# A decoder layer on one core: even key and value projections, self values by token tiles, output parts fetched three ahead

## The chip, the core and the metric

The kernel runs on one core of a Trainium2 chip. The metric is device time in microseconds from the start to the end of one execution; the median of several executions is compared. A core has five engines with a queue of instructions each, worked off in order: TensorE (PE in the profile; its weight loads are the row PEld), VectorE (DVE), ScalarE (ACT), GpSimd (POOL) and SyncE (SP). SP computes nothing here: it issues nearly all DMAs, and a DMA that has to wait for a buffer holds up all DMAs behind it on that queue.

## The reference, cut to what matters

One layer: self attention, cross attention, a mixture of experts, each added to its input and normalised. 16 sequences of 100 tokens, width 512, all in float32.

```python
x = layernorm(x + self_attention(x))             # 16 heads of 32, causal, softmax
x = layernorm(x + cross_attention(x, context))   # 16 query heads of 128, 4 key/value heads,
                                                 # context 16 x 361 x 512, q and k rms-normalised
x = layernorm(x + moe(x))                        # router picks 2 of 8 experts (512 x 512, silu), projection, rms norm
```

## The kernel before, in words

**Products.** Large float32 matrices are held as a pair, a rounded high part and the rest. `mm3` (lines 145 to 147) computes one product as three: high x high, low x high, high x low. `mmk` runs it over the four 128-row pieces of a 512-wide contraction, so that one 128 x 512 result costs 12 matmuls. `split` (lines 132 to 141) makes a pair: ACT (or DVE) casts the high part, DVE or POOL subtracts to get the low part.

**Order.** The program is written in one order, but a scheduler places each engine's instructions by its own estimate of times; it can move work of a later stage forward as soon as the memory of its tiles is free. Tiles come from pools that are opened and closed; a pool opened after others have been closed reuses their memory, and an instruction that writes into it waits until the last reader of what lay there before is done. `in_turn` and `keep_in_program_order` pin some instructions.

**Self attention** (0 to about 207 us): four groups of 4 sequences (400 tokens), 4 units of 4 heads in each group, 16 units in all. `self_v` computes values with one `mmk` for each sequence (100 tokens as weights, 512 columns), copies them by ACT from the accumulator to `V[g, r]`, and `self_attend` uses those as weights. The dictionary `extra`, filled by `at(unit, step, ...)`, puts other work between the steps of a unit: projections of the next units, values of the next group (units 2 and 3 of a group), splits of weight rows, and at the end the first output projections (`b_fetch`, `b_split`, `b_out`, `b_xT`; five tiles before the stage closes).

**Query stage** (about 207 to 440 us): output projection of self attention, layernorm, queries for cross attention, stored to DRAM (`qd`).

**Cross attention** (about 440 to 1087 us): 16 sequences x 4 key/value heads g, 64 units. A unit computes scores of the next unit (`x_scores`: three products of 362 columns for each of 4 heads, softmax over DVE, ACT, DVE, POOL), transposes its own probabilities in three chunks (`x_turn`) and multiplies them with the values (`x_attend`). Beside it `kv_project(b + 1, g)` projects keys and values of the next sequence, one chunk of 128 context rows in each of units g = 0, 1, 2; unit 3 has none. Keys are rms-normalised and transposed (`kv_turn`), values split into a spare weight slot. In every third unit a row of the output weights is fetched (`f_wo`) and split at once (`load_row`). The result goes to DRAM as `od`.

**Output projection of cross attention** (`acc`): 52 parts (13 tiles of 128 tokens x 4 heads g); `d_part` multiplies the four query heads of a part with 512 rows of output weights, 12 matmuls. `d_load(i + 1)` fetches the next part's `of` from `od` into pool `d_in` (two buffers) and splits it right away, one part ahead of its use. The last three tiles are done head by head. Between the parts lie `d_norm` (add, layernorm, store), `d_turn` (transposes for the router), `d_logits`, the routing (`choose`, `settle`, `slots`, on DVE and with small products), and `load_expert`, which fetches and splits the four rows of an expert's weights in one go, at parts 8, 16, 24 and 32 and for the other experts when a slot of output weights comes free.

**Experts and end**: `e_gather` collects tokens by an indirect DMA on POOL into the four `xs` buffers of pool `k_x` (`xsp`), which is opened after the attention's pools have been closed; then expert products, the final projection and norms.

Of the kernel before, what the change touches and what calls it, by code (L numbers as in the profile page):

```python
# [9 lines left out]
FP = mybir.dt.float32  # L10
# [7 lines left out]
B, S, D = 16, 100, 512  # L18
# [10 lines left out]
GB = 4  # L29
NG = B // GB  # L30
GT = GB * S
TT = [(t, min(128, T - t)) for t in range(0, T, 128)]
EPS_LN = 1e-5
EPS_RMS = 1e-6
# [28 lines left out]
def tile_decoder_layer(  # L63
    ctx: ExitStack,
    tc: tile.TileContext,
    x: bass.AP,
    xT: bass.AP,
    ctxT: bass.AP,
    mask: bass.AP,
    wqT: bass.AP,  # L70
# [25 lines left out]
    def pool(stack, name, bufs=1, **k):  # L96
        return stack.enter_context(
            tc.tile_pool(name=name, bufs=bufs, reuse_waits="tile", **k)
        )
# [124 lines left out]
    w1 = pool(a_l, "a_1", 1)  # L224
    w2 = pool(a_l, "a_2", 2)
    w3 = pool(a_l, "a_3", 8)
    ps.append(pool(a_l, "ps_a", 2, space=PSUM))
    ps_s = pool(a_l, "ps_s", 1, space=PSUM)

# [68 lines left out]
        split(*chunk("q", c), nc.scalar, nc.gpsimd)  # L298
        split(*chunk("k", c), nc.scalar, nc.gpsimd)

    def self_v(g, r):
        pv = bank("mm" if g else "t", [S, D], f"pv_{g}_{r}")
        mmk(
            pv,
            lambda k: xg[g][:, k, r * S : (r + 1) * S],
            lambda k: units["wv_s"][:, k, :],
        )
        V[g, r] = w1.tile([S, D], FP, name=f"v_{g}_{r}", tag="v", bufs=8)
        nc.scalar.copy(V[g, r], pv)

    def self_q(g, c):
        cc = slice(c * 128, (c + 1) * 128)
# [84 lines left out]
    def self_attend(g, c):  # L397

        av = bank("t", [128, GB, S], f"av_{g}_{c}")
        prev = None  # L400

        for r in range(GB):
            for j in (3, 0, 1, 2):
                h = c * 128 + 32 * j
                ins = nc.tensor.matmul(
                    av[32 * j : 32 * j + 32, r, :],
                    V[g, r][:, h : h + 32],
                    PT[g, c, j][:, r, :],
                    start=True,
                    stop=True,  # L410
                    tile_position=(0, 32 * j),
                )
                prev = in_turn(ins, prev)
        o = w2.tile([128, GT], FP, name=f"o_{g}_{c}", tag="o")
        nc.scalar.copy(o, av.rearrange("p r s -> p (r s)"))
        nc.sync.dma_start(o1d[g][:, c], o)
# [57 lines left out]

    ROW = {}

    def fetch_row(name, s, src, k):
        units[name] = slot_of(s)
        f = stage.tile([128, D], FP, name=f"f_{name}_{k}", tag="f")
        tc.keep_in_program_order(nc.sync.dma_start(f, src[:, k]))  # L480
        ROW[name, k] = f

# [11 lines left out]
    for u, (g, c) in enumerate(heads4):  # L494
        if u + 2 < NU:
            if u < 2:
                at(u, 0, split_chunk, u + 2)
            at(u, 0, self_k, *heads4[u + 2])
            at(u, 2, self_q, *heads4[u + 2])
        if g + 1 < NG:  # L500
            if c == 0:
                at(u, 1, fetch_x, g + 1)
                for k in range(2):
                    at(u, 3, split_x, g + 1, k)
            if c == 1:
                for k in range(2):
                    at(u, 1, split_x, g + 1, 2 + k)
            if c > 1:
                for r in range(2):
                    at(u, 1 + 2 * r, self_v, g + 1, 2 * (c - 2) + r)  # L510

    rows = [("wo_s", 3, kp(woT), k) for k in range(KC)]
    rows += [("wq_0", 4, Wqg[0], k) for k in range(KC)]
# [12 lines left out]
        at(i // 4, i % 4, behind, split_row, "wq_3", k)  # L526

    AHEAD = 5
    at(10, 0, b_open)
    for t, i in enumerate((44, 48, 52, 54, 58)):  # L530
        at(i // 4, i % 4, b_fetch, t)
        i += 2 if t == AHEAD - 1 else 4
        at(i // 4, i % 4, behind, b_split, t)
    for t, i in enumerate((51, 55, 59, 61, 62)):
        at(i // 4, i % 4, b_out, t)
    for t, i in enumerate((57, 60, 63)):
        at(i // 4, i % 4, b_xT, t)
# [1 line left out]
    self_q(0, 0)  # L539
    self_k(0, 0)  # L540
    self_scores(*heads4[0])
    self_v(0, 0)
    split_chunk(1)
    for r in range(1, GB):
        self_v(0, r)
    self_q(0, 1)
    self_k(0, 1)
    for u, unit in enumerate(heads4):
# [134 lines left out]

    spare = [slot_of(s)[:, k] for s in (4, 5) for k in range(KC)]

    def kv_project(b, i):
        c0, n = CH[i]
        if i == 0:
            K[b] = pair(w2, [128, NKV, SP], f"kT_{b}", tag="kT")
            nc.gpsimd.memset(K[b].h[:, :, SE:].bitcast(FP), 0.0)  # L690
            nc.gpsimd.memset(K[b].l[:, :, SE:].bitcast(FP), 0.0)
        ct = CT.pop((b, i))
        m = b * len(CH) + i
        pk = bank("mm", [128, D], f"pk2_{b}_{i}")
        mmk(pk[:n], lambda k: ct[:, k, :n], lambda k: wk[:, k, :])
        ks = w0.tile([128, D], FP, name=f"ks_{b}_{i}", tag="ks")
        nc.vector.tensor_tensor(ks[:n], pk[:n], bk_bc[:n], ALU.add)
        pv = bank("mm", [128, D], f"pv2_{b}_{i}")
        mmk(pv[:n], lambda k: ct[:, k, :n], lambda k: wv[:, k, :])
        VS[b, i] = spare[m % 6]  # L700
        split(VS[b, i][:n], pv[:n])
        kr = ks[:n].rearrange("p (h d) -> p h d", d=HD2)
        ss = small.tile([128, NKV], FP, name=f"kss_{b}_{i}", tag="kss")
        sq = w0.tile([128, HD2], FP, name=f"ksq_{b}_{i}", tag="sq", bufs=1)
        for h in range(NKV):
            nc.vector.tensor_tensor_reduce(
                out=sq[:n],
                in0=kr[:, h, :],
                in1=kr[:, h, :],
                scale=1.0,  # L710
                scalar=0.0,
                op0=ALU.mult,
                op1=ALU.add,
                accum_out=ss[:n, h : h + 1],
            )
        rs = rms_scale(ss[:n], n, NKV, f"k_{b}_{i}")
        nc.gpsimd.tensor_tensor(
            kr, kr, rs[:n].unsqueeze(2).to_broadcast([n, NKV, HD2]), ALU.mult
        )
        KS[b, i] = kr  # L720

    def kv_turn(b, i):
        c0, n = CH[i]
# [74 lines left out]
    for i in range(len(CH)):  # L798
        if i == 2:
            split_ctx(0, 2)  # L800
        kv_project(0, i)
        kv_turn(0, i)
    x_load(0, 1)
    for h in range(GR):
        x_scores(0, 0, h)
    order = [(b, g) for b in range(B) for g in range(NKV)]
    OT, X1 = {}, {}

    def d_open():
        kv_l.close()  # L810
        inp["d"] = pool(d_i, "d_in", 2)

    TAIL = 3
    parts = [(t, g) for t in range(NT - TAIL) for g in range(NKV)]
    parts += [(t, g) for g in range(NKV) for t in range(NT - TAIL, NT)]

    def d_load(i):
        t, g = parts[i]
        n = TT[t][1]
        p = inp["d"]  # L820
        of = p.tile([128, GR, 128], FP, name=f"of_{t}_{g}", tag="of")
        nc.sync.dma_start(of[:, :, :n], od[t][:, g * GR : (g + 1) * GR, :n])
        OT[t, g] = pair(p, [128, GR, 128], f"ot_{t}_{g}", tag="ot")
        split(OT[t, g][:, :, :n], of[:, :, :n], low=nc.vector if i % 2 else nc.gpsimd)

    def d_part(i, among={}):

# [34 lines left out]
    for i, (b, g) in enumerate(order):  # L862
        if b == B - 1:
            if g == 0:
                d_open()
                d_load(0)
            for j in range(HEAD * g, HEAD * (g + 1)):
                d_load(j + 1)
                d_part(j)
                if parts[j][1] == NKV - 1:  # L870
                    d_norm(parts[j][0])
        if b + 1 < B:
            if g == 0:
                fetch_ctx(b + 1)
                split_ctx(b + 1, 0)
            if g < len(CH):
                kv_project(b + 1, g)
            if g + 1 < len(CH):
                split_ctx(b + 1, g + 1)
        if i + 2 < len(order):  # L880
# [24 lines left out]
    ctx.enter_context(fin)  # L905
    k1 = pool(fin, "k_1", 1, side="right")
    xsp = pool(fin, "k_x", 4, side="right")
    gs = ExitStack()
    gw = pool(gs, "gate", side="right")
    d_l = ExitStack()  # L910
# [423 lines left out]

    raw = w1.tile([128, 2, D], FP, name="raw")

    def load_expert(e, last=False):
        for k in range(KC):
            if last and k > 1:
                f = raw[:, k - 2]  # L1340
            else:
                f = stage.tile([128, D], FP, name=f"f_e_{e}_{k}", tag="f")
                tc.keep_in_program_order(nc.sync.dma_start(f, kp(expert_w[e])[:, k]))
            split(
                slot_of(e)[:, k],
                f,
                nc.vector if last and k == 1 else nc.scalar,
                nc.vector if last and k else nc.gpsimd,
            )

    for i in range(HEAD * NKV, len(parts)):
        t, g = parts[i]
        if i + 1 < len(parts):
            d_load(i + 1)
        among = {}
        if t < NT - TAIL:
            if g == 1:
                d_turn(t - 1)
            if g == 3:
                among = d_logits(t - 1)  # L1360
            if g == 0 and t in (2, 4, 6, 8):
                load_expert(early[t // 2 - 1])
        elif t > NT - TAIL and g == 0:
            if t < NT - 1:
                d_turn(NT - TAIL - 1)
# [5 lines left out]
        if g == NKV - 1:  # L1371
            with tc.high_priority(offset=URGENT if t >= NT - TAIL else 0):
                d_norm(t)
        if t == NT - 1 and g < NKV - 1:
            load_expert(wo_slot[g])
        if (t, g) == (CUT, 0):
            nc.sync.dma_start(raw, kp(expert_w[wo_slot[3]])[:, 2:])
        if t % 3 == 0 and t <= CUT and g == 3:
# [3 lines left out]
        if (t, g) == (CUT, 3):  # L1382
            settle(0, CUT)
            slots(0, EARLY, CUT)
        if (t, g) == (NT - 1, 1):
            for k in range(4):
                e_gather(k)
    d_i.close()
    ck_l.close()
    load_expert(wo_slot[3], True)  # L1390
    e_turn(0)
    e_turn(1)
    e_product(0, d_logits(NT - TAIL))
# [436 lines left out]
```

## Time and profile before

| | us |
|---|---|
| median of 6 runs | 1415.05 (1411.93 to 1422.0) |
| profiled execution, its time | 1421.13 |
| its span, first to last instruction | 1419.3 |
| PE busy in the span | 1340.7 (94%) |
| DVE, ACT, POOL busy | 938.9, 757.5, 713.3 |
| mean granted clock of PE | 0.972 |

How to read it: times are those of one execution. A matmul is pipelined: its record is longer than the distance to the next one's start, so that a sum of records is more than the time they take. In a row of a timeline the bracket at the end says how long the engine sat idle before the instruction, and what ended that wait. In a row of waits stand the waiting engine and line, what it waited for, then the sum in us, how often, and the longest. In a table of stretches each engine has its busy time and, in brackets, its number of instructions; PEclk is the mean granted clock in that stretch.

### The profile page before, as it was taken

The page shows a single profiled execution, that of the slowest core. Times are in us where ns is not written, and L with a number is a line of the kernel's source. Part 1 is how long each engine was busy: PE and PEld are TensorE (multiplying, and loading weights), DVE is VectorE, ACT ScalarE, POOL GpSimd, SP SyncE. Part 2 cuts the span into 40 slices and gives each one's busy share as a digit, 9 for nine tenths or more (in the row PEclk, how much of TensorE's full clock was granted, in tenths as well). Part 3 has the DMA queues.
Part 4 walks back from the last instruction along what each step waited for, and adds up shares of the span by engine and source line. Part 5 has one row for each costly group of instructions (what it writes and reads, how often), then busy time and mean ns, then how long its engine had stood idle before and what let it go on. Part 6 is the DMA issues. An engine that isn't in the chain of part 4 may idle for free.

```text
span 1419.3 us, 25131 instructions
## 1 busy us (share of the span) xinstructions
PE 1340.7 (94%) x7952; PEld 1111.7 (78%) x7952; DVE 938.9 (66%) x2932; ACT 757.5 (53%) x1899; POOL 713.3 (50%) x839
## 2 busy tenths in 40 slices
PE   8999989999999999999999999999999898998895
PEld 7888868887778888888888778888888675686783
DVE  5776577766456777777677676776754557764587
ACT  4666653444445666666566556666654233333356
POOL 6877663344245555555455455554554445532630
PEclk9999989999999999999999999999999999899997
DMA  5231254555552223333333123322445554678874
GB/s 158 72 93 52 72 155 120 120 96 110 97 102 66 47 66 74 70 78 69 76 69 76 43 64 77 76 64 55 105 106 159 189 163 149 194 230 242 261 243 144
DMA packets 197872, 159.79 MB, mean 113 GB/s; under 512 B 133322, under 2 KB 152878, under 8 KB 197742
## 3 DMA queue, kind: packets, MB, share of 16 engines
q1 hardware_dynamic: 187904, 137.83, 37.1%
q0 software_dynamic: 4576, 14.95, 3.6%
q10 hardware_dynamic: 5262, 5.41, 1.3%
q8 instruction: 65, 1.06, 0.3%
q14 instruction: 65, 0.53, 0.1%
HBM read 107.16 MB, written 50.99 MB: 111 GB/s over the span
## 4 chain that ended last, share of the span: by engine, by line
PE 63%; DVE 13%; DMA 13%; ACT 5%; issue 3%; POOL 2%; SPq 1%; ACTq 0%; DVEq 0%; POOLq 0%
PE pv L145 4%; PE pv L146 4%; PE pv L147 3%; PE ptp L767 3%; PE pk L145 3%; PE pk L147 3%; PE pk L146 3%; DMA qd<-qTb 3%; PE s L145 3%; PE pq L145 3%; PE pq L147 3%; PE pq L146 3%; DMA f_wo<-in_Wo 3%; PE s L147 3%; PE s L146 2%
## 5 line engine op out<-in xcount | busy, mean ns | idle before, releaser
L759 POOL TENSOR_SCALAR p<-p,sums 100x361 f32<-100x361 f32 x256 | 146.5, 576 | 103.4 <-DVE sums L758 92.3
L746 DVE CUSTOM_DVE_ANT_0 p<-s,nmask 100x361 f32<-100x361 f32 x256 | 133.1, 527 | 67.4 <-PE s L147 59.1
L757 ACT ACTIVATE p<-p,nm 100x361 f32<-100x361 f32 x256 | 153.1, 601 | 40.1 <-DVE nm L746 36.8
L140 DVE TENSOR_TENSOR pT_l<-ptp,pT_h 128x400 fp32r<-128x400 f32 (+1 forms) x192 | 107.5, 568 | 56.4 <-ACT pT_h L137 55.8
L145 PE MATMUL pq<-WH 128*128 128x512 f32 (+2 forms) x272 | 107.1, 394 | 5.5 <-DVE WH L139 5.5
L767 PE MATMUL ptp<-ident,p 100*128 100x100 f32 (+1 forms) x768 | 107.2, 251 | 0.0
L137 ACT CAST pT_h<-ptp 128x400 fp32r<-128x400 f32 (+1 forms) x192 | 91.2, 486 | 29.7 <-PE ptp L767 29.1
L767 PEld LDWEIGHTS ptp<-ident,p 100*128 100x128 f32 (+1 forms) x768 | 95.3, 151 | 13.2 <-POOL p L759 2.3
L140 POOL TENSOR_TENSOR cT_l<-cf,cT_h 128x512 fp32r<-128x512 f32 (+1 forms) x48 | 54.3, 1132 | 100.2 <-ACT cT_h L137 98.2
L146 PE MATMUL pq<-WL,WH 128*128 128x512 f32 (+2 forms) x272 | 104.5, 384 | 0.0
L147 PE MATMUL pq<-WH,WL 128*128 128x512 f32 (+2 forms) x272 | 104.2, 383 | 0.0
L147 PE MATMUL acc<-WH,ot_l 128*128 128x512 f32 (+1 forms) x208 | 86.3, 416 | 7.8 <-DVE ot_l L140 6.2
L145 PE MATMUL acc<-WH,ot_h 128*128 128x512 f32 (+1 forms) x208 | 85.8, 413 | 6.7 <-ACT ot_h L137 6.7
L145 PE MATMUL s<-kT_h,WH 128*100 128x362 f32 x256 | 88.3, 355 | 2.1 <-ACT kT_h L137 2.1
L145 PE MATMUL av<-pT_h,WH 128*128 128x400 f32 (+1 forms) x192 | 77.2, 402 | 12.2 <-ACT pT_h L137 11.7
L147 PE MATMUL s<-kT_h,WL 128*100 128x362 f32 x256 | 84.8, 331 | 0.0
L146 PE MATMUL acc<-WL,ot_h 128*128 128x512 f32 (+1 forms) x208 | 84.5, 406 | 0.0
L146 PE MATMUL s<-kT_l,WH 128*100 128x362 f32 x256 | 84.2, 329 | 0.0
L614 POOL TENSOR_TENSOR qs<-qs,r_q 128x512 f32<-128x512 f32 (+1 forms) x52 | 54.0, 1068 | 58.9 <-DVE r_q L169 47.7
L140 POOL TENSOR_TENSOR WL<-qf,WH 128x400 fp32r<-128x400 f32 x64 | 67.3, 1051 | 31.2 <-ACT WH L137 27.7
L145 PE MATMUL pv<-WH,cT_h 128*128 128x512 f32 (+1 forms) x192 | 79.7, 415 | 1.3 <-DVE WL L140 1.3
L145 PE MATMUL pk<-WH,cT_h 128*128 128x512 f32 (+1 forms) x192 | 78.3, 408 | 0.3
(337 smaller groups left out, 4012.6 us busy)
## 6 DMA issues: line engine op xcount, KB each, us to landing
qf<-qd SPq DMA_DIRECT2D x64, 200.0 KB, 3.1
of<-od SPq DMA_DIRECT2D x48, 256.0 KB, 3.8
cf<-in_ctxT SPq DMA_DIRECT2D x16, 722.0 KB, 4.3
eb<-in_expert_b SPq DMA_DIRECT2D x32, 256.0 KB, 4.4
ysd<-h SPq DMA_DIRECT2D x32, 256.0 KB, 4.5
f_e<-in_expert_w SPq DMA_DIRECT2D x30, 256.0 KB, 4.6
f_wq<-in_Wq SPq DMA_DIRECT2D x16, 256.0 KB, 3.4
f_wo<-in_Wo SPq DMA_DIRECT2D x16, 256.0 KB, 4.8
```

The source lines that it names most:

```text
L137: ins = nc.scalar.copy(dst.h, src)
L140: low.tensor_tensor(dst.l, src, dst.h.bitcast(FP), ALU.subtract)
L145: nc.tensor.matmul(out, a.h, b.h, start=start, stop=False)
L146: nc.tensor.matmul(out, a.h, b.l, start=False, stop=False)
L147: nc.tensor.matmul(out, a.l, b.h, start=False, stop=stop)
L614: nc.gpsimd.tensor_tensor(qr[:, hs, :], qr[:, hs, :], rs[:n, hs].unsqueeze(2).to_broadcast([n, GR, HD2]), ALU.mult,)
L746: nc.vector.tensor_tensor_reduce(out=p, in0=sc[:, :SE], in1=nmask, scale=1.0, scalar=BIG, op0=ALU.add, op1=ALU.min, accum_out=nm,)
L757: nc.scalar.activation(p, p, AF.Exp, bias=nm, scale=-1.0, accum_out=sh)
L759: nc.gpsimd.tensor_scalar(p, p, sh, 1.0, ALU.mult, ALU.mult)
L767: nc.tensor.transpose(pt[:n, h, :], probs[h][:, c0 : c0 + n], ident[:S, :S])
```

## The change

Three parts.

1. *Self values by token tiles.* For groups 1 to 3 a group's 400 tokens are taken as three tiles of 128; the remaining 16 tokens of the three groups (48 in all, a new input `xlT`) are projected in one go. As sequences begin at multiples of 100, rows of a tile are then moved by DMA into the `V[g, r]` that they belong to. Group 0 stays as it was. To keep the pool `a_x` open, `b_open` and the first output fetches move from unit 10 and 11 to unit 12.
2. *Even projections.* `kv_project` is cut into `k_project` and `v_project`. Keys of the next sequence stay at g = 0, 1, 2; values go to g = 0, 2, 3.
3. *Output parts and expert rows.* `d_load` is cut into `d_fetch` (the DMA) and `d_load` (the split). After attention the fetches run three parts ahead, in the `xs` buffers of `xsp`. Expert rows are fetched up to four ahead (in `stage` and in the buffers of `d_in` that the parts no longer use) and split one by one, every second part. The first gathers are issued from part 48 instead of 45.

```diff
-    def self_v(g, r):
-        pv = bank("mm" if g else "t", [S, D], f"pv_{g}_{r}")
-        mmk(pv, lambda k: xg[g][:, k, r * S : (r + 1) * S], lambda k: units["wv_s"][:, k, :])
-        V[g, r] = w1.tile([S, D], FP, name=f"v_{g}_{r}", tag="v", bufs=8)
-        nc.scalar.copy(V[g, r], pv)
+    def self_v_last():
+        pv = bank("mm", [NL, D], "pv_last")
+        mmk(pv, lambda k: xg["l"][:, k, :], lambda k: units["wv_s"][:, k, :])
...
+    def self_v(g, t):
+        pv = bank("mm", [128, D], f"pv_{g}_{t}")
+        mmk(pv, lambda k: xg[g][:, k, t * 128 : (t + 1) * 128], lambda k: units["wv_s"][:, k, :])
...
+        nc.scalar.copy(vt, pv)
+        a = S if t == 0 else t * 128
+        while a < (t + 1) * 128:
+            r, o = divmod(a, S)
+            m = min(S - o, (t + 1) * 128 - a)
+            nc.sync.dma_start(V[g, r][o : o + m], vt[a - t * 128 : a - t * 128 + m])
+            a += m
+        if t == 2:
+            a = (g - 1) * REST_V
+            nc.sync.dma_start(V[g, GB - 1][S - REST_V : S], V["l"][a : a + REST_V])
...
-    at(10, 0, b_open)
-    for t, i in enumerate((44, 48, 52, 54, 58)):
+    at(12, 0, b_open)
+    for t, i in enumerate((48, 50, 52, 54, 58)):
...
             if g < len(CH):
-                kv_project(b + 1, g)
+                k_project(b + 1, g)
+            for j in ((0,), (), (1,), (2,))[g]:
+                v_project(b + 1, j)
...
+    def d_fetch(i):
+        t, g = parts[i]
+        n = TT[t][1]
+        p, tag = inp["of"]
+        f = p.tile([128, D], FP, name=f"of_{t}_{g}", tag=tag)
+        OF[i] = f = f.rearrange("p (h n) -> p h n", n=128)[:, :, :n]
+        nc.sync.dma_start(f, od[t][:, g * GR : (g + 1) * GR, :n])
...
+    inp["of"] = xsp, "xs"
...
+    ROWS = 4
+    def e_rows(i):
+        while rows_out[0] < len(erows) and split_at[rows_out[0]] <= i:
+            e, k = erows[rows_out[0]]
+            in_turn(split_row(f"e_{e}", k), split_last[0])
+            rows_out[0] += 1
+            e_fetch()
...
+    begun = HEAD * NKV + 1
+    e_fetch()
     for i in range(HEAD * NKV, len(parts)):
         t, g = parts[i]
+        while begun < min(i + 4, len(parts)):
+            d_fetch(begun)
+            begun += 1
         if i + 1 < len(parts):
             d_load(i + 1)
+        e_rows(i)
...
-            if g == 0 and t in (2, 4, 6, 8):
-                load_expert(early[t // 2 - 1])
...
-        if t == NT - 1 and g < NKV - 1:
-            load_expert(wo_slot[g])
...
-        if (t, g) == (NT - 1, 1):
+        if i == len(parts) - 4:
             for k in range(4):
                 e_gather(k)
```

## The prediction

> **What bounds the kernel now.** I read first the busy time by stretches of the span, cut where the stages change. PE is the TensorE, PEclk the granted clock as a share of full speed.
>
> ```profile
> core 0: us, PE busy (x) PEld busy (x) DVE busy (x) ACT busy (x) POOL busy (x), PEclk, DMA share, GB/s
> ...
> 40.00:180.00 140.00, 139.71 (x1442) 117.56 (x1438) 91.87 (x220) 87.86 (x255) 105.68 (x118) 1.00 0.24 73
> 180.00:220.00 40.00, 34.21 (x271) 27.27 (x269) 26.84 (x58) 19.50 (x49) 20.69 (x21) 0.87 0.57 177
> ...
> 440.00:995.00 555.00, 536.34 (x3008) 458.00 (x3007) 397.08 (x1512) 351.46 (x952) 295.34 (x406) 0.98 0.29 67
> 995.00:1090.00 95.00, 94.00 (x509) 80.76 (x508) 53.34 (x155) 54.33 (x135) 45.84 (x55) 1.00 0.48 118
> 1090.00:1186.00 96.00, 87.49 (x418) 68.95 (x417) 50.70 (x171) 29.27 (x65) 42.48 (x40) 0.96 0.58 179
> 1186.00:1216.00 30.00, 23.14 (x84) 16.20 (x83) 26.70 (x57) 9.18 (x16) 19.10 (x15) 0.89 0.44 142
> ```
>
> Self attention (40 to 180) is PE from end to end. Its close (180 to 220) loses 5.8 us idle and 0.13 x 40 = 5.2 us of clock. Cross attention (440 to 995) has 18.7 us of PE gaps. The last batch of attention with the first output parts (995 to 1090) is full. The other parts (1090 to 1186) lose 8.5 us to gaps and 0.04 x 96 = 3.8 us to the clock. From 1186 to 1216 it is VectorE (DVE), 26.7 of 30, that is full, not PE.
>
> Then the timeline of PE for the price of one product. Columns: start, duration, engine, line.
>
> ```profile
> 99.27 0.39 PE L146 MATMUL pv<-WL,WH 128*100 128x512 f32 x1
> 99.50 0.39 PE L147 MATMUL pv<-WH,WL 128*100 128x512 f32 x1
> 99.73 0.39 PE L145 MATMUL pv<-WH 128*100 128x512 f32 x1
> ```
>
> A 512-column product lasts 0.39 us but the next starts 0.23 us later: 0.23 is the price. (`acc` of 128 columns of weights starts 0.23 apart too, so 128 instead of 100 tokens cost nothing more.)
>
> Then the waits: cross attention's gaps, and the output parts' stall.
>
> ```profile
> PE av L145 <- ACT pT_h L137: 11.7, 12, 2.5
> PE av L146 <- DVE pT_l L140: 4.0, 19, 0.5
> ```
> ```profile
> 789.07 0.62 ACT L137 CAST WH<-f_wo 128x512 fp32r<-128x512 f32 x1 [3.35 <-DMA f_wo<-in_Wo]
> ```
> ```profile
> 1119.74 0.62 ACT L137 CAST WH<-f_e 128x512 fp32r<-128x512 f32 x1 [6.13 <-DMA f_e<-in_expert_w]
> ```
> ```profile
> 1122.23 0.80 PE L145 MATMUL acc<-WH,ot_h 128*128 128x512 f32 x1 [3.13 <-ACT ot_h L137]
> 1122.82 0.63 PE L146 MATMUL acc<-WL,ot_h 128*128 128x512 f32 x1
> ```
>
> ScalarE (ACT) stands in front of a weight row that has not landed, and the cast that PE needs is queued behind it; after the 3.13 us gap the products last 0.63 us instead of 0.39.
>
> **Part 1, self values by token tiles.** Groups 1 to 3 have 4 x 12 products each, 144; after, 3 x 12 each and one set of 12 for the 3 x 16 remaining tokens, 120. 24 x 0.23 = **5.5 us**, on a PE with 0.3 us idle in 140. Added: one fetch, 3 small splits, 18 DMAs on SP that move rows of V between partitions; ACT loses two copies of 0.59. POOL, next in line, does 105.7 us in 140, so it stays covered. The added wait is PE's `av` for moved V. No SBUF-to-SBUF move is in the trace; nearest rows are the stores `o1d<-o`, median 2.3 us, and `qd<-qTb`, 5.1 us; I take 4 with up to 2 in SP's queue. In the built order (each engine's sequence, no times) 48 products of 400 columns (0.18 apart), 6 transposes of four (0.29), scores and one `av` stand between the last value tile and the first `av` that needs it: 8.6 + 1.7 + 1.6 = 11.9 us. Covered; without cover, at most 6 us in each of three groups. Behind these DMAs on SP stand the `f_wo_s` and `f_wq` rows, a unit ahead of use. At the close, the built order puts some 13 us of PE work between the last scores and their transposes instead of 9, because the output fetches moved and the units closed up: of 5.8 idle and 5.2 clock I count 1.5 back. Sum **-7**, ends -11 and -2.
>
> **Part 2, even projections.** No product is added or taken. The built order shows that the scheduler had already spread them: V of chunk 1 stood in the fourth unit, V of chunk 2 in the next batch's first. K2 and V1 change places, V2 goes one score later. Around the awkward `f_wo` rows PE's work between the `o` that frees SP and the stalled `av` is what it was (6.2 us in four cases, 5.0 in two). So **0**; ends -4 (a fifth of the gaps) and +2 (transposes that lose V2 as cover; at 635.2 POOL had finished all four `p`, the transposes ran at 636.1).
>
> **Part 3, output parts and expert rows.** Here the built order moves most. Before, 203 of 624 `acc` products run before the last `av` of attention (at 1087.3), under the softmax of batch 15. After, 60: the fetch buffers of part 5 onward lie in `xsp`, opened when attention's pools close, and the fetch of part 5 waits for attention's very last product; that of part 6 waits until the last two `od` stores have landed (they had that memory). Moving 143 x 0.23 = 32.9 us from under attention to after it is free as long as PE is the bound in both. The price is what opens up:
> - Batch 15 alone: a unit is 12 score products at 0.165 us, 12 transposes at 0.07 and 9 `av` at 0.18, some 4.5 us of PE; ACT has 4 exponentials at 0.59, 3 casts at 0.38, `o` and `qf` at 0.5, some 4.5 as well. So latencies show, most of all in the last two units, which have no scores to compute. I take 5 us (2 to 9).
> - The drain: `o` 0.7, two stores 0.9, one fetch 0.4 on SP, then `of` landing. Row: minimum 2.6, median 3.7, maximum 6.4; near 1092 it took 4.2. Cast 0.6, so PE resumes 7 us (5 to 9) after its last product. Part 6: stores 4.9 to land, then 4.2 and 0.7: 1.5 us more (0 to 3). Behind these fetches on SP stand those of parts 7 to 9 and the last expert's rows, none needed sooner.
> - Clock: the 3.13 us gap above had products at 0.63 from 1122 on; a 7 us gap should get at least that. 2.5 us (1.7 to 3.4).
> - Left in the loop: `chosen` 0.7 and little else, as fetches are 3 parts (8.4 us) ahead and rows 8 parts. 1 us (0.5 to 5).
>
> Gone: the gap of 1.0 at 1048, the 8.5, the 3.8. Up to the product that starts the routing (1185.7): 5 + 7 + 1.5 + 2.5 + 1 - 13.3 = **+3.7**. From there DVE leads:
>
> ```profile
> 1185.96 0.18 DVE L1115 COPY rank<-gb 128x24 f32<-128x24 f32 x1 [0.79 <-PE gb L1108]
> ```
> ```profile
> 1212.57 1.17 DVE L1247 TENSOR_TENSOR is_in<-seq,tile_of 128x288 f16<-128x288 f32 x1
> ```
> ```profile
> 1216.03 0.61 PE L1262 MATMUL gb<-is_in,named 128*128 128x11 f16 x18
> ```
>
> The chain takes 27.8 us; PE has only 7 parts x 2.8 = 19.6 to do in it. So the 6.9 us gaps of PE there are not to be won; only the 2.1 us by which PE is late: 3.7 - 2.1 = +1.6. Gathers wait for the index alone in the built order, as before. PE will stand some 8 us before the slot products (L1262) and run the two last parts at a low clock, largely under the gathers' 5.2 us: +0.4. Sum **+2**, ends -6 and +14.
>
> [...]
>
> **Sum.** -7 + 0 + 2 = -5 us. The profiled execution took 1421.13 (span 1419.3 and 1.8 around it): 1416.1. It lies 6.1 over the median of the six runs, 1415.05, so the forecast for the median is **1410.0**.
>
> **Rivals.**
> 1. *Drain and bare attention decide (slower).* At the upper ends (9, 9, 3, 3.4, 1) part 3 comes to +12 before the routing and +10 after it; with 3 to 4 us from self attention, 1421. For: no gap of PE in this span is as long as 7 us. Against: each is a sum of upper ends. It outweighs part 1 from a drain and unfilled time of 18 us together.
> 2. *Fetches win in full.* Attention closes up (2), drain 5, clock 1.7, loop 0.5, part 6 hidden: -4.1, after slack -6, with -8 from self attention: 1401. For: all gaps from 1090 to 1186 start at a landing. Against: the drain chain is made of rows.
> 3. *The first part doesn't show*: V lands late or POOL (76% of 140 us) becomes the bound; -2 in place of -7: 1415. Against: 11.9 us cover. That the even projections do nothing is in the forecast already.
>
> **Chances.** Forecast (1405 to 1415) 0.50, rival 1 0.20, rival 2 0.17, rival 3 0.13. A measurement of this kernel tells 0.3%, 4.2 us, from no change. Faster: all of rival 2 and 0.55 of the forecast, 0.45; slower: 0.19 of rival 1; the same 0.36. Range 1400 to 1421.
>
> **What would show it.** Right: `acc` starts its second tile only after the last `av`; a PE gap of 5 to 9 us there waiting for ACT `ot_h` behind DMA `of`; no wait of ACT for `f_e` afterwards; PE waiting for DVE `is_in` 6 to 10 us; 120 `pv` products outside group 0; cross attention within 4 us of now. Wrong: PE waits for V's DMAs in `av`, the drain is filled, or the DVE chain is much shorter than 27.8 us.

## The result, and the profile after

The changed kernel is **slower**, by 0.7%: the median of 20 runs is 1426.55 us (1420.31 to 1434.7), that of 46 runs of the kernel before 1416.62; the ratio is 1.0069, 95% interval 1.0054 to 1.0083. That is 9.9 us more, where 5 us less were forecast. The profiled execution has a span of 1431.8 us (1419.3 before), 12.5 us more. Chips differ (the kernel before had medians from 1402.2 to 1420.9 us in six groups of runs), so kernels are compared by their ratio to runs of the kernel before on the same chip.

The busy time by stretches, cut as before:

```profile
core 0: us, PE busy (x) PEld busy (x) DVE busy (x) ACT busy (x) POOL busy (x), PEclk, DMA share, GB/s
...
440.00:995.00 555.00, 532.29 (x2993) 457.37 (x2992) 391.56 (x1508) 346.58 (x948) 293.96 (x406) 0.98 0.30 67
995.00:1090.00 95.00, 80.72 (x434) 68.94 (x433) 47.62 (x154) 47.88 (x121) 39.38 (x56) 0.91 0.50 122
1090.00:1186.00 96.00, 94.62 (x450) 76.83 (x449) 48.36 (x151) 31.88 (x65) 45.95 (x35) 0.98 0.57 177
1186.00:1216.00 30.00, 24.50 (x104) 17.02 (x104) 24.54 (x60) 9.08 (x17) 14.50 (x13) 0.89 0.44 128
```

The output parts from 1090 to 1186, which lost 8.5 us to gaps before, now lose 1.4: what part 3 was to do there, it does. But the stretch ahead of them, full before (94.0 of 95), now lacks 14.3 us of PE and a tenth of the clock. PE's timeline shows one long gap in it (1.1 us more lie in short ones):

```profile
1052.88 0.35 PE L149 MATMUL av<-pT_h,WL 105*128 105x400 f32 x1
1066.46 0.80 PE L147 MATMUL acc<-WH,ot_h 128*128 128x512 f32 x1 [13.23 <-ACT ot_h L139]
```

This is the stand between attention's last product and part 5. The work of every kernel below was cut at the same instructions, and the lengths (us) of these stretches in the profiles set side by side. The cuts: the first transposes of probabilities in cross attention; the last transposes of its keys; the copy of `rank` that starts the routing chain (third of five); the last `acc` product; the copy of `rank` for the last three tiles (the fifth, here "the last count").

| profile | to first transposes | cross attention | to routing chain | to last `acc` | to last count | to the end |
|---|---|---|---|---|---|---|
| before | 441.3 | 591.0 | 153.7 | 36.6 | 29.6 | 167.1 |
| changed | 438.3 | 589.1 | 164.9 | 39.2 | 34.0 | 166.2 |
| before, second profile | 437.9 | 581.2 | 153.8 | 38.0 | 28.3 | 163.7 |
| self_alone | 433.2 | 581.4 | 151.6 | 35.4 | 33.2 | 168.8 |
| outputs_alone | 435.9 | 580.6 | 160.0 | 39.2 | 34.1 | 170.0 |
| rows_later | 437.1 | 578.8 | 158.1 | 40.0 | 32.0 | 167.7 |
| changed_pinned | 433.3 | 578.5 | 163.2 | 39.1 | 31.2 | 161.9 |
| hybrid_24_router | 435.3 | 576.8 | 145.1 | 39.4 | 40.1 | 161.2 |
| hybrid_repaired | 436.5 | 575.5 | 147.3 | 39.7 | 32.0 | 162.6 |
| self_pinned | 434.0 | 581.5 | 152.7 | 37.2 | 27.3 | 168.1 |
| self_pinned_wo2 | 435.3 | 569.5 | 152.1 | 37.1 | 29.1 | 164.8 |
| self_even_wo2 | 437.0 | 559.8 | 156.2 | 34.8 | 28.9 | 172.1 |
| hybrid_repaired_wo2 | 437.2 | 559.2 | 147.1 | 36.6 | 32.0 | 165.9 |

From before to changed: -3.0, -1.9, **+11.2**, **+2.6**, **+4.4**, -0.9. Each row is one execution, and two executions of the kernel before differ by 3.4 us in the first column and in the last and by 9.8 in the second, so only differences seen in several rows are used.

**How the stand came about.** SP's timeline over it:

```profile
1052.93 0.43 SPq L527 DMA_DIRECT2D f_e<-in_expert_w  x1
1053.47 0.84 SPq L916 DMA_DIRECT2D x<-x1d  x2
1055.85 1.83 SPq L847 DMA_DIRECT2D od<-o  x2
1057.72 0.50 SPq L916 DMA_DIRECT2D x<-x1d  x1
1058.44 7.35 SPq L881 DMA_DIRECT2D of<-od  x3
```
ScalarE's, over the same time:
```profile
1059.71 0.35 ACTq L990 DMA_DIRECT2D rb<-in_router_b  x1
...
1065.79 0.62 ACT L139 CAST ot_h<-of 128x512 fp32r<-128x512 f32 x1 [11.93 <-DMA of<-od]
```

The last `o` is ready at 1053.85 (1053.26 + 0.59), but its first store is issued at 1055.85 and its second at 1057.30; then comes an `x` fetch, then the fetch of part 5 at 1058.44. The semaphores in the trace say what these waited for. In the first profile of before the 667 DMAs of SP and ACT tell of their landing through eight semaphores, and the next use of a semaphore stands eight places further on in 637 of 659 cases (six to ten in the others); in all 576 pairs of such uses whose first landing is recorded in full, the second DMA was issued only after the first had landed. So it was here. Eight places ahead of the two stores stand the stores of the unit before (landed 1055.78 and 1057.29; the two were issued 0.07 and 0.01 us later), and eight ahead of the fetch of part 5 stands an expert row, the third of four issued from 1051.41 on (landed 1058.35, the fetch issued 0.09 us later). The chain of work that ended last, followed back from part 5, runs through that row (columns: start, length):

```profile
1052.46 5.90 DMA f_e<-in_expert_w
1058.37 0.03 SPq L881
...
1058.44 7.32 DMA of<-od
```

So the expert rows, which part 3 fetches early, stand in the queue ahead of the last stores; the fetch of part 5 waited for one of them, not for attention's last product (done at 1053.23). The second half of the stand is the landing: 7.3 us, at 1065.8, with 4.2 in my sum. The DMA engines were full meanwhile, but not with bytes (third column from the end: the clock; then DMA share; GB/s):

```profile
1056.00:1060.00 4.00, 0.00 (x0) 0.00 (x0) 0.00 (x0) 0.00 (x0) 0.00 (x0) 0.64 1.09 308
1060.00:1064.00 4.00, 0.00 (x0) 0.00 (x0) 0.00 (x0) 0.00 (x0) 0.00 (x0) 0.50 1.29 94
1064.00:1068.00 4.00, 1.54 (x6) 1.35 (x6) 0.69 (x1) 1.10 (x2) 0.00 (x0) 0.50 0.75 203
1068.00:1072.00 4.00, 4.00 (x13) 3.42 (x14) 0.17 (x1) 0.62 (x1) 2.55 (x2) 0.50 0.88 270
```

The packets were small: between 1058 and 1066, 1801 of 2358 were under 512 bytes (`od` stores and the router's weights). That these made the landing slow is argued from the share of 1.29 at 94 GB/s; no run here takes them away and keeps the stand. The clock column shows the rest of the price: 0.50 from 1060 on, and still 0.50 from 1068 to 1072, with PE full. The products last 0.63 us until 1073.9.

### The profile page after: what moved, and what is told of

Same layout as the page of the kernel before. It is cut to its first block, busy times and chain, and to the rows that moved or that the text cites. A ratio compares the mean times of both kernels' runs of the same rounds, so it can differ in the third digit from the quotient of the medians.

```text
span 1431.8 us, 25105 instructions
## 1 busy us (share of the span) xinstructions
PE 1336.0 (93%) x7928; PEld 1110.8 (78%) x7928; DVE 935.9 (65%) x2933; ACT 753.4 (53%) x1897; POOL 711.0 (50%) x840
## 4 chain that ended last, share of the span: by engine, by line
PE 62%; DMA 13%; DVE 12%; ACT 6%; issue 3%; SPq 2%; POOL 1%; ACTq 0%; DVEq 0%; POOLq 0%
DMA f_wo<-in_Wo 3%; PE pv L147 3%; PE pv L148 3%; PE pv L149 3%; DMA qd<-qTb 3%; PE acc L149 3%; PE acc L147 3%; PE acc L148 3%; PE ptp L822 3%; PE pk L147 3%; PE pk L149 3%; PE pk L148 3%; PE s L147 2%; PE s L148 2%; PE s L149 2%
## 5 line engine op out<-in xcount | busy, mean ns | idle before, releaser
L822 PE MATMUL ptp<-ident,p 100*128 100x100 f32 (+1 forms) x768 | 101.9, 252 | 0.0
L822 PEld LDWEIGHTS ptp<-ident,p 100*128 100x128 f32 (+1 forms) x768 | 92.3, 151 | 7.2
L764 POOL TENSOR_TENSOR ks<-ks,r_k 128x512 f32<-128x512 f32 (+1 forms) x48 | 49.9, 1041 | 93.6 <-DVE r_k L171 80.5
L142 POOL TENSOR_TENSOR WL<-qf,WH 128x400 fp32r<-128x400 f32 x64 | 67.3, 1052 | 40.3 <-ACT WH L139 40.1
L139 ACT CAST ot_h<-of 128x512 fp32r<-128x512 f32 (+1 forms) x52 | 31.4, 604 | 105.7 <-PE acc L148 78.2
```

The costliest lines, as they stand in the source:

```text
L139: ins = nc.scalar.copy(dst.h, src)
L142: low.tensor_tensor(dst.l, src, dst.h.bitcast(FP), ALU.subtract)
L764: nc.gpsimd.tensor_tensor(kr, kr, rs[:n].unsqueeze(2).to_broadcast([n, NKV, HD2]), ALU.mult)
L822: nc.tensor.transpose(pt[:n, h, :], probs[h][:, c0 : c0 + n], ident[:S, :S])
```

## The experiments

The **theory** I began with: the stand, with its 13.2 us and the half clock behind it, is the whole of the loss, and a kernel without it is faster than before. The **rivals**: what follows the stand (DVE's routing chain, the experts, landings) sets the time anyway; or part 1's saving does not last.

### Which part costs

`self_alone` is the kernel before with part 1, `self_and_even` with parts 1 and 2, `outputs_alone` with part 3. Edits against the changed kernel, in short:

```diff
 # self_alone, self_and_even: part 3 undone
-    inp["of"] = xsp, "xs"
-        while begun < min(i + 4, len(parts)):
-            d_fetch(begun)
+            if g == 0 and t in (2, 4, 6, 8):
+                load_expert(early[t // 2 - 1])
 # self_alone, outputs_alone: part 2 undone
+                kv_project(b + 1, g)
-                k_project(b + 1, g)
 # outputs_alone: part 1 undone
+    def self_v(g, r):
+        pv = bank("mm" if g else "t", [S, D], f"pv_{g}_{r}")
```

> Part 1 alone on the kernel before. Theory (the stand of TensorE at the end of attention made the loss, 13.2 us of gap and 3.9 us of half clock): the 24 products less show, minus what the close of self attention takes back; 3 to 5 us faster than before, a ratio near 0.997. Rival (part 1 does not show, because the close of self attention gives all of it back): 0 to 1 us, ratio 1.000.

> Parts 1 and 2, without part 3. Theory: part 2 is worth nothing, so the same as part 1 alone within 1.5 us. Rival (the moved value projections cost cross attention something): 2 us or more slower than part 1 alone.

> Part 3 alone on the kernel before. Theory (the stand of TensorE decides): 13 to 15 us slower than before, ratio about 1.010, with a gap of 10 us or more ahead of part 5 and some 7 us of half clock after it. Rival (part 3 costs 2 us as forecast and the loss is in the interplay with the other parts): ratio 1.001.

Measured: `self_alone` 1.0006 (0.9992 to 1.0020), `self_and_even` 1.0006 (0.9989 to 1.0023), `outputs_alone` **1.0092** (1.0070 to 1.0113), that is 12 to 13 us slower, with a gap of 11.26 us ahead of part 5. So the loss is part 3's, and part 2 shows nothing here (the intervals are some 2 us wide to either side). Part 1 does not show in the whole, 1.0006 where about 0.997 was expected: its rival held. What becomes of its saving is followed below.

### The stand

`rows_later` moves the first four expert rows behind the first parts' fetches. `hybrid_fetch` lets parts up to 17 use the old buffers, which are free while attention runs.

```diff
 # rows_later
     begun = HEAD * NKV + 1
-    e_fetch()
...
+        if i == HEAD * NKV + 1:
+            e_fetch()
 # hybrid_fetch
-    inp["of"] = xsp, "xs"
-        while begun < min(i + 4, len(parts)):
+    SWITCH = 18
+        while begun < min(i + (3 if begun < SWITCH else 4), len(parts)):
+            if begun == SWITCH:
+                inp["of"] = xsp, "xs"
             d_fetch(begun)
-                      erows[r][1], inp["d"] if r % 5 > 2 else stage)
+                      erows[r][1], inp["d"] if r >= 8 and r % 5 > 2 else stage)
```

> The changed kernel with one edit: the first four expert rows are fetched behind the first output parts instead of ahead of attention's last store. Theory (1 MB of rows and the small packets in the queues made part 5 land in 7.3 us instead of 4): the gap ahead of part 5 shrinks from 13.2 to about 10 us and the time falls by 2 to 4 us against the changed kernel, ratio to before 1.004 to 1.006. Rival (the chain of stores and the fetch's own latency make the stand): gap and time as in the changed kernel, ratio 1.007 to 1.009.

> The changed kernel, but output parts up to 17 are fetched two ahead into the two old buffers, which are free before attention ends, and only parts from 18 on into the gathers' buffers; the first eight expert rows stay in the staging pool, three ahead. In the built order 199 of 624 output products stand ahead of attention's last product again (60 in the changed kernel, 203 before). Theory: no stand at the end of attention; 14 to 18 us faster than the changed kernel, so 4 to 8 us faster than before, ratio 0.995 to 0.997. Rival (the routing chain on VectorE and the experts set the end, whatever the order of the parts): no more than 5 us faster than the changed kernel, ratio 1.003 or above.

> The kernel before, unchanged, for a profile on the same chip as the kernels beside it; both theories expect a span within 0.5% of the other runs of before here.

`before_again` gave the second profile of before in the table (span 1402.9 us). `rows_later`: 1.0086 (1.0057 to 1.0115). Its gap is 9.81 us, shorter than in the three other kernels with this stand (13.2, 11.3, 11.9). SP's timeline in `rows_later`, where `o` is ready at 1042.32, shows where the difference lies:

```profile
1042.35 0.92 SPq L847 DMA_DIRECT2D od<-o  x2
1043.45 7.64 SPq L881 DMA_DIRECT2D of<-od  x2
```

Without the rows ahead of them the two stores go out at once, and the fetch of part 5 follows 1.1 us after `o`, not 4.6 as in the changed kernel (3.4 and 4.0 in `outputs_alone` and `changed_pinned`). The fetch still takes 7.4 us to land (1043.45 to 1050.82), so the theory, which had put the slow landing down to the rows, was wrong, though the gap it named came. The stretch to the routing chain, 158.1 us, is the shortest of the four kernels with the stand, but the time shows no gain; a gain of up to 2 us would lie within the intervals.

`hybrid_fetch`: 1.0036 (1.0017 to 1.0054). The stand at 1053 is gone, but a second one is there; PE's timeline of `hybrid_fetch`:

```profile
1076.99 1.09 PE L1003 MATMUL ptx<-ident,x 128*128 128x128 f32 x4 [3.85 <-DVE x L183]
1080.73 1.85 PE L1022 MATMUL gb<-rw,x2f 128*128 128x8 f32 x8 [2.65 <-DMA rw<-in_router_w]
```

The first gap ends with a layernorm, the second with the landing of the router's weights. These lie, like the fetch buffers of the changed kernel, in a pool that is opened when attention's pools close, and PE had no part left to do while they landed: 17 parts were done, and the products of the next start at 1086.49. Two edits follow: the switch at part 24 with all expert rows in the staging pool, three ahead (`hybrid_24`), and beside it the router's weight and bias in a pool open from the start (`hybrid_24_router`).

```diff
-    SWITCH = 18
+    ROWS = 3
+    SWITCH = 24
 # hybrid_24_router
-    rw = gw.tile([128, KC, NE], FP, name="rw")
+    rw = const.tile([128, KC, NE], FP, name="rw")      # in the query stage; rb too
```

> The hybrid with the switch at part 24 instead of 18, and all expert rows in the staging pool, three ahead, so that the two old buffers serve parts alone. Theory (the hybrid lost its gain to a second stand, 3.85 and 2.65 us of gap and 6.8 us of half clock near 1077, where TensorE had no further part and waited for the router): with more parts on hand most of it goes; 4 to 8 us faster than the first hybrid, ratio to before 0.997 to 1.001. Rival (the routing chain on VectorE sets the time from there on): no change against the first hybrid, ratio 1.003 to 1.005.

> The same, with the router's weight and bias in a pool that is open from the start and fetched in the query stage. Theory: the wait of TensorE for the router's landing (2.65 us in the first hybrid) goes, 1 to 4 us faster than hybrid_24, ratio to before 0.995 to 1.000. Rival (the routing chain on VectorE): no change against hybrid_24.

`hybrid_24`: 1.0049 (1.0023 to 1.0075), no gain, though its profile reaches the routing chain 3.5 us earlier than `hybrid_fetch`. `hybrid_24_router`: 1.0017 (0.9996 to 1.0038). There the routing chain starts 15.6 us before that of the second profile of before (1157.3 against 1172.9), and the last `acc` product 14.3 us before; but at the last count only 2.5 us are left. The theory of the stand alone had fallen: taking the stand away brings the routing chain forward, but most of that is paid back later. PE's timeline of `hybrid_24_router` after the last `acc`:

```profile
1196.63 0.42 PE L149 MATMUL acc<-WH,ot_l 128*64 128x512 f32 x1
...
1200.46 1.11 PE L1373 MATMUL pte<-ident,xs 128*128 128x128 f32 x4 [2.54 <-ACT x2f L1009]
1204.20 1.11 PE L1002 MATMUL ptx<-ident,x 128*128 128x128 f32 x4 [2.63 <-DVE xsT_l L142]
1207.30 0.66 PE L1002 MATMUL ptx<-ident,x 64*128 64x64 f32 x4 [1.98 <-issue]
...
1209.19 1.20 PE L147 MATMUL ph<-WH,xsT_h 128*128 x2
```

The scheduler, which goes by its own estimate of times, has put the transposes of tiles 11 and 12 (`ptx`) ahead of the first expert products (`ph`). Both wait, and the products behind them with them. In the kernel before the products stand first. A second exchange is in `self_alone`, `outputs_alone` and the changed kernel: the count of the last three tiles stands behind expert product 4 (counted from 0) instead of ahead of it, and the last count comes 33 to 34 us after the last `acc`, not 28 to 30.

### The order at the end

`self_pinned` is `self_alone` and `changed_pinned` the changed kernel with the count pinned; `hybrid_pinned` is `hybrid_24_router` with that pin and tile 11's transposes behind the first expert product; `hybrid_repaired` also pins the count of tile 9 behind it. In short, with plain names:

```diff
 # all four
+            if i == 4 and k == 0:
+                in_turn(first_product, last_count)
 # hybrid_pinned, hybrid_repaired
+            if k == 0 and t == NT - 2:
+                in_turn(transpose, last_product_of_ph_0)
 # hybrid_repaired
-            choose(CUT, CUT + 1)      # at part 46
+        choose(CUT, CUT + 1)          # after ph_0, its count in_turn behind it
```

> Part 1 alone, with one order pinned: the product that counts the choices of the last three tiles stands ahead of the fourth expert product again, as in the kernel before (in part 1 alone the scheduler had put it 12 products later). Theory (part 1 saves about 4 us, and that exchange in the experts' order gives them back, since the second routing chain hangs on it): 3 to 6 us faster than part 1 alone, ratio to before 0.996 to 0.998, and the last count comes about as long after the last output product as before (28 to 30 us, 33 in part 1 alone). Rival (the exchange is harmless and part 1 saves nothing that lasts): ratio 1.000 again.

> hybrid_24_router with two orders pinned: the same count ahead of the fourth expert product, and the transposes of tile 11 behind the first expert product instead of ahead of it. Theory (the hybrid reaches its last output product 14 us earlier than before and loses 12 of them up to the last count, because these products stand in the wrong order): 4 to 8 us faster than hybrid_24_router, ratio to before 0.995 to 0.998. Rival (the landing of gathers and expert rows sets that stretch, whatever the order): no change, ratio 1.001 to 1.003.

> The changed kernel with one order pinned: the count of the last three tiles' choices ahead of the fourth expert product. Theory (the exchange costs the changed kernel 4 to 5 us between the last output product and that count, beside the stand): 2 to 5 us faster than the changed kernel, ratio to before 1.003 to 1.006, and 28 to 30 us from the last output product to the last count in place of 34. Rival (landings set that stretch): ratio 1.007 to 1.009 and 33 us or more.

> hybrid_24_router with three orders pinned: the first expert product ahead of tile 11's transposes and ahead of the count of tile 9, and the count of the last three tiles ahead of the fourth expert product. Theory (order): the last output product some 12 to 14 us earlier than before and no more than 32 us from there to the last count (34 in hybrid_pinned, with 6 us of wait for a count; 40 in hybrid_24_router); ratio to before 0.993 to 0.997. Rival (landings of gathers and rows): TensorE waits for gathers or expert rows in place of the count, ratio 1.000 or above.

`self_pinned`: 0.9991 (0.9974 to 1.0007). `self_pinned_wo`, which was to split cross attention's weight rows later, turned out to have the very same built order, because the scheduler moved the split back to where it had been; so it says nothing on the rows and is a second measurement of `self_pinned`: 0.9977 (0.9958 to 0.9995). The two centre on 0.998, some 2 us faster than before (the first interval reaches 1), and the last count comes 27.3 and 29.3 us after the last `acc` (33.2 unpinned). `hybrid_pinned`: 1.0007 (0.9991 to 1.0023), not the 0.995 to 0.998 of its theory; its first expert product now waited 6.1 us behind the count of tile 9 (`hybrid_pinned_wo`, again the same built order: 1.0013, 0.9993 to 1.0034).

> self_pinned with another edit: a row of output weights in cross attention is fetched as before but split one unit later. Theory (the stalled row is what holds up the cast that TensorE needs): most of the 14 to 18 us of gaps and 2 to 4 us of half clock of cross attention go, 8 to 16 us faster than self_pinned, ratio to before 0.985 to 0.992. Rival (the gaps come from the shape of a unit, not from the landing): within 2 us of self_pinned.

> hybrid_pinned with the same edit in cross attention. Theory: the two add up, 8 to 16 us faster than hybrid_pinned, ratio to before 0.982 to 0.990. Rival: within 2 us of hybrid_pinned.

`changed_pinned`: 1.0039 (1.0014 to 1.0063), 4 us less than the changed kernel by the ratios, which come from different chips and have intervals that overlap, and 31.2 us to the last count in place of 34.0; the stand is still there (11.94 us). `hybrid_repaired`: **0.9953** (0.9933 to 0.9972), as forecast, and by the medians on one chip 13.9 us faster than `changed_pinned` (1396.51 against 1410.44). From the last `acc` to the last count it takes 32.0 us where `hybrid_24_router` took 40.1. So the order, not the landings, made most of the loss after the last `acc`. Not all of it: in `hybrid_repaired` PE waits for the cast of an expert row, for whose landing DVE itself stood 1.4 us:

```profile
1211.52 1.20 PE L147 MATMUL ph<-WH,xsT_h 128*128 x2 [6.71 <-DVE WH L141]
```

### Cross attention's weight rows

The gaps in cross attention were the largest loss of PE ahead of the experts in the profile of before (18.7 us), and part 2 was priced by them. Here the split of a row is pinned one unit after its fetch:

```diff
-            load_row(f"wo_{w}", wo_slot[w], Wo4[w], k)
+            if i % 3 == 2:
+                fetch_row(f"wo_{w}", wo_slot[w], Wo4[w], k)
+            elif i % 3 == 0:
+                in_turn(split_row(f"wo_{w}", k), last_cast_of_probabilities)
```

> self_pinned with the split of each output weight row of cross attention pinned behind the last cast of probabilities of the next unit, one unit (about 8 us) after its fetch. Theory (the split ahead of its landing makes cross attention's gaps): ScalarE no longer waits for the row, the 14 us of gaps in cross attention fall to 6 or less, 6 to 12 us faster than self_pinned, ratio to before 0.990 to 0.994. Rival (the gaps come from the shape of the unit; another cast is late instead): gaps stay above 10 us, ratio 0.997 to 0.999.

> hybrid_repaired with the same pinned split in cross attention. Theory: both gains add, ratio to before 0.985 to 0.991. Rival: as hybrid_repaired.

> self_pinned_wo2 with part 2 added, part 3 as in the kernel before. Theory (once the rows do not stall, the even projections save PE the small stalls inside the units; start to last key transpose was 996 us in hybrid_repaired_wo2 and 1005 us in self_pinned_wo2): some 6 to 9 us faster than self_pinned_wo2, ratio to before 0.980 to 0.983. Rival (the difference came from the repaired part 3): as self_pinned_wo2, ratio 0.985 to 0.989.

> The same kernel as hybrid_repaired_wo2, beside self_even_wo2 on one chip. Theory (part 2 made the difference, the repaired part 3 is worth little on top): within 3 us of self_even_wo2. Rival (the repaired part 3 made it): 5 us or more faster than self_even_wo2; ratio to before about 0.982 in both cases.

`self_pinned_wo2`: **0.9870** (0.9836 to 0.9905), against 0.998 for `self_pinned` on another chip, more than the 0.990 to 0.994 of the theory. A wait of ScalarE in `self_pinned` (us in total, times, longest):

```profile
ACT WH L139 <- DMA f_wo<-in_Wo: 24.6, 16, 3.0
```

has no counterpart in `self_pinned_wo2`. Cross attention by stretches, first in `self_pinned`, then in `self_pinned_wo2`:

```profile
440.00:995.00 555.00, 541.24 (x3061) 462.60 (x3060) 404.76 (x1540) 359.61 (x973) 301.85 (x414) 0.99 0.29 70
```
```profile
440.00:995.00 555.00, 549.13 (x3130) 469.69 (x3129) 414.19 (x1564) 367.30 (x991) 307.52 (x421) 1.00 0.29 72
```

PE is idle for 5.9 us in place of 13.8, and the mean clock there is 1.00 in place of 0.99. `hybrid_repaired_wo2`: **0.9824** (0.9790 to 0.9857). Beside `hybrid_repaired` on one chip it is 16.3 us faster by the medians (1380.21 against 1396.51), and this one edit is all that lies between the two. It is 6.6 us below `self_pinned_wo2` there (1386.79). On another chip `self_even_wo2`, which has parts 1 and 2 and the old part 3, gives 0.9768 (0.9746 to 0.9789), and the same `hybrid_repaired_wo2` beside it 0.9766 (0.9741 to 0.9792). The same kernel, then, had 0.9824 on one chip and 0.9766 on the other, so a difference of 0.6% between ratios from different chips shows little by itself. The repaired part 3 adds nothing that can be told on top of the others (medians 1385.93 and 1388.14), and the 6.6 us are mostly part 2's: start to last key transposes takes 1004.8 us in `self_pinned_wo2`, 996.8 in `self_even_wo2`. That part 2 is worth some 4 us or more once the rows do not stall is worked out from two chips and one profile each, not measured by itself.

`hybrid_repaired_wo2` and `self_even_wo2` beat both kernels; the second is the simpler one.

## Why the prediction was wrong

The step that failed first is the drain of part 3, put at 7 us: it took 13.2, because with four expert rows ahead of it in the queue the fetch of part 5 was issued 4.6 us after `o`, and because it took 7.3 us to land where 4.2 were counted. Two more went wrong: the way from the routing to the last `acc`, put at -1.7 (+2.6), and the order of the experts, put at nothing (+4.4). Step by step, with the profile of the changed kernel:

- **Part 1, -7: the products were saved, the close took some back, and the end the rest.** PE does its 120 products 0.23 us apart, as expected. The moves of V cost nothing, as predicted: 2.3 us to land (3.5 at most) where I took 4 and had 11.9 us of cover, and no `av` waits for one. The last score product of self attention starts at 173.6 to 175.0 us in all 17 profiles with part 1 and at 183.1 to 183.3 in the three without; 12 output products (2.8 us) and 32 `av` moved behind it, which leaves about the 5.5 us. But the close, from which I counted 1.5 back, lost more: the last `av` of self attention starts at 201.6 to 204.0 against 205.6 to 207.0, some 3 us earlier. At the first transposes of cross attention the two sets overlap (431.6 to 438.3, and 435.9 to 441.3). In the medians nothing is left, as the exchanged count took 4 to 5 us; with the count pinned, about 2 us are. Where the rest went is open: the last stretch takes 168 us in `self_alone` and `self_pinned`, 164 and 167 in the profiles of before, which is no more than it varies.
- **Part 2, 0: right for this kernel** (`self_and_even` against `self_alone`, both 1.0006). That cross attention's stalled rows hid what it is worth is likely by the last group of runs, not shown.
- **Part 3 up to the routing, +3.7: the mechanism was right, the drain mis-sized.** Measured +11.2. The terms: drain 13.2 in place of 7; clock 3.9 in place of 2.5 (products from 1066.5 to 1074.2 at half speed); part 6's wait 0 in place of 1.5; the rest of the loop 3.1 (a gap of 1.4 and 1.7 of clock) in place of 1; the bare batch 3.4 in place of 5 (0.8 of gaps; the rest is what remains of the sum); what went, 12.5 (13.3). The 2.5 for the clock, with its range of 1.7 to 3.4, was an estimate of mine that no run shows; the whole stretches of half clock in the first profile of before last 3.41 or 6.83 us, and the one here lasts 17.07, of which PE stood for 9.4. In the drain, I had put `o`, two stores, fetch and landing end to end, as if nothing stood ahead of them. From `o` to the issue of the fetch it took 4.6 us, where the stores' 0.9 were counted, since the two stores and the fetch were issued only after the DMAs eight places ahead of them had landed (1055.78, 1057.29 and, an expert row, 1058.35), and the built order had four expert rows there; `rows_later`, without them, took 1.1. And the landing took 7.3 us, longer than the longest of `of` before, 6.4. The second wait that I had named, part 6 behind the landing of the last store, is in the trace (1064.94), but half-speed products covered it.
- **From the routing on, -1.7: wrong.** I gave 2.1 us back, since DVE's chain leads and PE was late. In fact the stretch to the last `acc` grew by 2.6 us. The chain was longer (29.6 us from `rank` to `is_in`, 27.8 before; 1.7 of it wait for a cast by ACT), and PE stood, as predicted in sum, for 8.9 us; but it waited for two splits of parts that are queued in DVE's chain, not for `is_in`:

```profile
1203.94 0.69 PE L149 MATMUL acc<-WH,ot_l 128*64 128x512 f32 x1 [5.50 <-DVE ot_l L142]
...
1220.17 0.50 PE L149 MATMUL acc<-WH,ot_l 128*128 128x512 f32 x1 [3.36 <-DVE ot_l L142]
```

- **The experts: a missing step.** I compared the built order up to the gathers and took the rest as unchanged. It was not: the stretch with one count behind an expert product is 4.4 us longer, of which the pin gives 2.8 back, and in `hybrid_24_router` the stretch with its exchanges is 12 us longer than in the second profile of before, of which the pins give back 8.
- **What was right:** no wait of ScalarE for `f_e` is left, and that for `of` fell from 29.1 to 17.2 us, of which the stand is 11.9. The wait for `f_wo`, which the change does not touch, was 30.8 us in the first profile of before and 24.3 in the second, and is 39.6 here:

```profile
ACT WH L139 <- DMA f_wo<-in_Wo: 39.6, 16, 4.2
...
ACT ot_h L139 <- DMA of<-od: 17.2, 4, 11.9
```

The first rival, drain and bare attention, was the nearest. It asked for 18 us of drain and unfilled time; 16.6 came. The clock cost 3.9 for its 3.4, and what it left out, the longer way to the last `acc` and the order of the experts, did the rest.

## What to carry to other kernels

A prefetch is only as early as the memory it lands in: buffers that a late stage frees turn "three ahead" into "after the last product". It is also only as early as its place in the queue: here the fetch of part 5 was issued 0.09 us after the landing of an expert row eight places ahead, 4.6 us after `o` where it took 1.1 without the rows, so fetches that nobody needs yet can hold up the one that everybody waits for. Price such a drain issue by issue, with what stands ahead in the queue and with the landing under that traffic, not by the median row. Where a scheduler decides, compare the built order to the very end: a change that shifts its estimates can exchange two instructions hundreds of us away. And look for the large losses in the profile of before, here the split ahead of its landing (16 us), before moving work around them.

## What was not expected of the hardware

- After the stand of 13.2 us the products ran at half speed for 7.7 us more (0.63 us each until 1073.9; the trace's clock record rises at 1074.2). In the three other kernels with this stand it was 8.0, 6.9 and 6.3 us (`outputs_alone`, `changed_pinned`, `rows_later`), so it was no accident of one execution. In the first profile of before and in that of the changed kernel every whole stretch of half clock is one, two or five times 3.41 us long; the one here is the only one of five (17.07 us, from 1057.1 on), and the longest in the first profile of before is of two (6.83). What set its length no run here shows: PE was busy without a gap from 1067.3 to 1070.7 too, for 1.6 us of it with the router's products of 8 columns, and the clock stayed at 0.50.
- Chips differ by more than the change is worth: the kernel before had medians from 1402.2 to 1420.9 us in the six groups of runs. Cross attention took 591.0 us in one profile of before and 581.2 in the other, with 30.8 and 24.3 us of wait for the rows' landings. The kernels that split the rows later lie within 8 us of each other on both chips they ran on (1380.2 to 1388.1), where before lay at 1403.6 and 1420.9.
